# Two pieces of the next stage's start are issued in the third batch of an attention, not near its end

## The chip, the cores and the metric

The kernel runs on one NeuronCore of one Trainium2 chip. The metric is the device time of one execution in microseconds (us), as a median over executions. All arithmetic is in float32.

An instruction belongs to one engine: PE (TensorE, matrix products and transposes), DVE (VectorE), ACT (ScalarE), POOL (GpSimd) or SP (the queue that issues the DMAs). Each engine takes its instructions in one fixed order; an instruction that waits for another engine holds up everything behind it on its own engine.

## The reference

There are 8 sequences of 512 rows with 256 columns. Four blocks follow each other, each added to its input; the second and the fourth use the same weights.

```python
x = x + attn_a(layernorm(x))      # softmax attention with a low-rank key/value
x = x + ffn(layernorm(x))         # two layers: local attention, then a gated feed-forward
x = x + attn_b(layernorm(x))      # 16 heads of 16 columns, causal
x = x + ffn(layernorm(x))
```

The block around the change is `attn_b`. For every head and every pair of rows it computes

```python
dot    = q @ k.T
den    = |q|^2 + |k|^2 - 2 * dot + 1e-6
scores = dot * dot / den          # then the causal mask, softmax, times v, output projection
```

and `layernorm` of the block after it is `(x - mean) / sqrt(var + 1e-5)` over the 256 columns of each row.

## The kernel before, in words

The 8 sequences ("batches" in the code) are worked on in two groups of four. For a group, six kinds of stage follow each other: `attention_a`, then twice (local attention `attention_f`, `feedforward`), then `attention_b`, then twice again (`attention_f`, `feedforward`). So `attention_b` is run twice in the program, once for each group, and is followed each time by the first `attention_f` of the last block.

**How stages overlap.** Each stage gives a `head()`, a generator whose pieces prepare its first work, and a `run(ahead)`. While a stage runs, it calls `ahead()` at places of its own choosing; each call issues one piece of the next stage's head. When the pieces are used up, further calls do nothing. `ahead()` decides only where the instructions stand in the engines' orders; no call waits for anything by itself.

**The head of `attention_f`** runs its steps -5 to -1, one for each `ahead()` call, so five calls do something:

- Step -5: `statistics` of the first batch, that is `row_statistics`: for each of 4 row tiles one `bn_stats` (L276) and one `bn_aggr` (L277) on DVE into `st_f..` and `mv_f..`, then on POOL one `tensor_scalar` (L266) and one power (L267) that make `rstd_f..`.
- Step -4: `rows` of the first batch, that is `normalize_rows`: 4 `tensor_scalar` (L283) on DVE that write the tile `y_..` from `x`, `mv` and `rstd`.
- Step -3: `started`: a memset, 4 transposes of the first half of the columns on PE (`pht_f..`, L295) into the one PSUM buffer tagged `mm`, and a DVE copy out of it (`hT_f..`, L506).
- Step -2: the second half of the columns, the query, key and value products (`pqk_f..`, `pv_f..`, L510), the rotation (L538, L541, L552).
- Step -1: normalized and turned keys, the second tile's products, and `row_statistics` of the second batch.

**The steps of `attention_b`.** The work is cut into 22 units for each batch (2 for the first 128 rows, 4, 8 and 8 for the next), 88 for the four batches. Step `s` of 93 does a part of several units at once, in an order that is written out by hand in `each_part` and kept on every engine by `order_keeper`:

- PE: the products `den_b` of unit s and `dot_b` of unit s-1 (L1197), the first half of the transposes `ppt_b` of unit s-3 (L1269, into the `mm` buffer), a piece of other work or a filler product (`idle_b`, L1174), on odd steps the products with v (`o_b`, L1284) of two units, then the second half of the transposes.
- DVE: `refine` of unit s-1 (`r_b`, L1220), `highest` of unit s-2 (two L1239 for each pair of heads), copy of the first half of the transposes (`pt_b`, L1274), `error` of unit s (`t_b`, L1216), copy of the second half, then a piece if there is one.
- ACT: `inverse` of unit s (logarithm and exponential, `r_b` by the helper line L241), the square of `dot_b` (L1226), `exponentials` of unit s-2 (`num_b`, also L241).
- POOL: the mask of unit s-1 (L1232) and the sign of the row maxima of unit s-2 (`most_b`, L1249), for which the exponentials wait.

While batches 0, 1 and 2 are at work, the units of the batch after them are prepared by pieces in between: products `pu_b` (L1085, L1098), their squares on ACT (L1095) and their copies (L1111 on DVE, L1117 on ACT). The last batch has no such work beside it; there the places are filled with `idle_b`.

Where `ahead()` is called after a step, its DVE and POOL instructions are bound to come after that step's last one on the same engine. The PE and ACT instructions of the head are placed by the scheduler.

Of the kernel before, what the change touches and what calls it, by code (L numbers as in the profile page):

```python
# [46 lines left out]
def kernel(  # L47
# [56 lines left out]
    def part(flat, at, shape):  # L104

        n = int(np.prod(shape))
        view = flat[:, at : at + n]
        if len(shape) == 2:
            view = view.rearrange("p (k n) -> p k n", n=shape[1])
        return view, at + n  # L110
# [948 lines left out]
    def attention_b(batches, g, norms_b, state):  # L1059
# [107 lines left out]
        def whole(piece):  # L1167
            for part in piece[1:]:
                if part:
                    part()  # L1170
# [177 lines left out]
        def steps(ahead):  # L1348
# [5 lines left out]
            each, count = len(units) // len(batches), len(units)  # L1354
# [76 lines left out]
            for step in range(count + 5):  # L1431
                if step % each == 0:
                    with kept_order():
                        while prologues or norms:
                            whole((norms or prologues).popleft())
                    following = step // each + 1
                    if following < len(batches):
                        prologues = deque(stacks_and_values(batches[following]))
                elif step == 6:
                    norms.extend(Piece(False, dve=lambda part=part: part(batches[-1])) for part in norms_b)  # L1440
                made = len(nc.cur_bb.bb.instructions)
                with kept_order():
                    each_part(step)
                if step > count - 4:

                    after = len(nc.cur_bb.bb.instructions)
                    ahead[0]()
                    every = nc.cur_bb.bb.instructions
                    for engine in (mybir.EngineType.DVE, mybir.EngineType.Pool):
                        own = [i for i in every[made:after] if i.engine == engine]  # L1450
                        for i in every[after:] if own else ():
                            if i.engine == engine:
                                tc.add_manual_dep(i, own[-1].name, ISSUE_ORDER, reason="head")
                yield
# [3 lines left out]

        follower = []
        rest = steps(follower)  # L1460

        def head():
# [133 lines left out]
```

## Time and profile before

| | |
|---|---|
| median of 3 runs | 4423.52 us (4421.06 to 4423.76) |
| the profiled execution | 4422.09 us |
| its span, first to last instruction | 4420.3 us |
| mean granted TensorE clock | 0.993 |
| busy share of the span: PE, DVE, ACT, POOL | 95%, 70%, 61%, 27% |
| `attention_b` of the first group, about 1015 to 1500 us: PE, DVE, ACT, POOL busy of 485 us | 428.5, 443.3, 418.2, 123.9 us |
| `attention_b` of the second group, about 3213 to 3690 us: of 477 us | 423.5, 438.6, 415.2, 123.5 us |

How to read the views. Times are us from the span's start unless they are marked ns. A row of the timeline has start, length, engine, line of the kernel, operation, output<-inputs by the program's names, and how often it is repeated; in brackets stands how long the engine was idle before it and what ended that. PEld is the loading of PE's weights. A row of the windows has, after the stretch and its length, the busy time of PE, PEld, DVE, ACT and POOL (with the number of instructions), the TensorE clock that was granted (1.00 is full speed), the DMA engines' share and GB/s. The chain of waits follows back from the last instruction, at each step to what released it, and lists the pieces in order of time. The next instruction of an engine may start shortly before the one before it is shown to end, so the cost of an instruction in a busy stretch is the distance from its start to the next one's.

### The profile page before, as it was taken

The numbers are of one execution on the slowest core, as the hardware profiler recorded it, in microseconds if no ns is written. First come the engines' busy times: TensorE is split into PE (matmuls) and PEld (weight loads), VectorE is DVE, ScalarE is ACT, GpSimd is POOL, SyncE is SP. The second block draws the span as 40 slices with busy tenths as digits, with TensorE's granted clock in tenths as the row PEclk, the third lists the DMA queues.
The fourth block names the chain that finished last, engine by engine and source line by source line (L and its number), as shares of the span: only waits on it lengthen the run. The fifth ranks groups of instructions, "written<-read, shape, count | busy, mean of one in ns | idle before, by whom it ended". The sixth has DMA issues, their size and how long they took to land.

```text
span 4420.3 us, 70595 instructions
## 1 busy us (share of the span) xinstructions
PE 4195.3 (95%) x26580; PEld 2536.5 (57%) x26580; DVE 3100.1 (70%) x7497; ACT 2699.3 (61%) x6316; POOL 1175.5 (27%) x1220
## 2 busy tenths in 40 slices
PE   9999999999888899999999999999999888999999
PEld 5666556655555465566566665565545554655655
DVE  6678737747999786377466786377479997863773
ACT  6777517716898675176167675276178996742761
POOL 0014214312222342143200242243122223422431
PEclk9999999999999999999999999999999999999999
DMA  2000000000000000000100000000000000000000
GB/s 82 1 22 4 23 3 23 3 24 20 2 1 1 20 4 7 4 22 13 53 30 1 20 3 24 22 4 23 5 21 1 2 1 20 4 6 23 3 4 23
DMA packets 51092, 63.36 MB, mean 14 GB/s; under 512 B 6336, under 2 KB 45504, under 8 KB 50752
## 3 DMA queue, kind: packets, MB, share of 16 engines
q1 hardware_dynamic: 50752, 58.85, 4.1%
q8 instruction: 211, 3.46, 0.3%
q14 instruction: 129, 1.06, 0.1%
HBM read 46.28 MB, written 4.19 MB: 11 GB/s over the span
## 4 chain that ended last, share of the span: by engine, by line
PE 74%; DVE 14%; ACT 9%; issue 1%; POOL 1%; DMA 0%; SPq 0%; POOLq 0%; ACTq 0%; DVEq 0%
PE pu_g1x L932 3%; PE pu_g0x L932 3%; PE pu_g0y L932 3%; PE pu_g1y L932 3%; PE s_a L389 3%; PE o_a L425 3%; PE ppt_a L414 3%; PE pqk_f1x L510 2%; PE pqk_f1y L510 2%; PE pqk_f0y L510 2%; PE pqk_f0x L510 2%; DVE pt_b L1274 2%; PE ppt_b L1269 2%; DVE r_b L1220 2%; PE pu_b L1085 1%; DVE num_b L1239 1%
## 5 line engine op out<-in xcount | busy, mean ns | idle before, releaser
L1269 PE MATMUL ppt_b<-ident,num_b 128*128 128x128 f32 x1280 | 227.5, 294 | 93.1 <-DVE pt_b L1274 63.3
L1269 PEld LDWEIGHTS ppt_b<-ident,num_b 128*128 128x128 f32 x1280 | 139.7, 144 | 279.3 <-ACT num_b L241 92.6
L241 ACT ACTIVATE num_b<-num_b,most_b 128x512 f32<-128x512 f32 (+3 forms) x512 | 280.6, 553 | 21.4 <-POOL most_b L1249 21.2
L1232 POOL TENSOR_TENSOR num_b<-num_b,causal 128x256 f32<-128x256 f32 x256 | 200.8, 797 | 258.9 <-ACT num_b L1226 258.9
L1274 DVE COPY pt_b<-ppt_b 128x512 f32<-128x512 f32 (+1 forms) x352 | 224.4, 637 | 36.8 <-PE ppt_b L1269 35.3
L1239 DVE CUSTOM_DVE_ANT_0 num_b<-num_b,r_b 128x512 f32<-128x512 f32 (+3 forms) x512 | 238.1, 512 | 3.7 <-POOL num_b L1232 3.7
L241 ACT ACTIVATE p_a<-s_a,nm_a 128x512 f32<-128x512 f32 x256 | 173.7, 683 | 105.0 <-DVE nm_a L393 101.9
L1216 DVE TENSOR_TENSOR t_b<-den_b,r_b 128x1024 f32<-128x1024 f32 (+1 forms) x176 | 197.3, 1121 | 25.9 <-ACT r_b L241 25.6
L1197 PE MATMUL den_b<-st_b,st_b 18*128 18x384 f32 (+3 forms) x1024 | 207.0, 476 | 7.5 <-ACT yT_b L1075 4.1
L1220 DVE SCALAR_TENSOR_TENSOR r_b<-t_b,r_b 128x1024 f32<-128x1024 f32 (+1 forms) x176 | 208.6, 1185 | 0.2
L393 DVE TENSOR_REDUCE nm_a<-s_a 128x2 f32<-128x1024 f32 x128 | 156.4, 1223 | 70.4 <-PE s_a L389 70.4
L241 ACT ACTIVATE r_b<-den_b 128x1024 f32<-128x1024 f32 (+1 forms) x176 | 165.8, 942 | 52.5 <-PE den_b L1197 30.1
L241 ACT ACTIVATE p_f0y<-p_f0y,nm_f0y,rn_f0y 128x256 f32<-128x256 f32 (+1 forms) x256 | 143.8, 563 | 80.6 <-DVE nm_f0y L649 80.5
L241 ACT ACTIVATE p_f1y<-p_f1y,nm_f1y,rn_f1y 128x256 f32<-128x256 f32 (+1 forms) x256 | 143.8, 563 | 80.6 <-DVE nm_f1y L649 80.5
L1197 PE MATMUL dot_b<-st_b,st_b 16*128 16x384 f32 (+3 forms) x1024 | 191.6, 475 | 0.0
L241 ACT ACTIVATE p_f1x<-p_f1x,nm_f1x,rn_f1x 128x256 f32<-128x256 f32 (+1 forms) x256 | 143.8, 564 | 76.0 <-DVE nm_f1x L649 75.9
L241 ACT ACTIVATE p_f0x<-p_f0x,nm_f0x,rn_f0x 128x256 f32<-128x256 f32 (+1 forms) x256 | 143.8, 564 | 75.3 <-DVE nm_f0x L649 75.2
L407 ACT ACTIVATE p_a<-p_a,sums_a 128x512 f32<-128x512 f32 x256 | 171.9, 719 | 26.5 <-DVE sums_a L405 26.5
L552 POOL TENSOR_TENSOR ro_f1x<-ro_f1x,rs_f1x 128x512 f32<-128x512 f32 x64 | 80.2, 1276 | 360.8 <-DVE rs_f1x L541 144.8
L552 POOL TENSOR_TENSOR ro_f0x<-ro_f0x,rs_f0x 128x512 f32<-128x512 f32 x64 | 80.2, 1275 | 360.6 <-DVE rs_f0x L541 144.8
L241 ACT ACTIVATE r_b<-r_b 128x1024 f32<-128x1024 f32 (+1 forms) x176 | 172.5, 980 | 5.7
L1226 ACT ACTIVATE num_b<-dot_b 128x1024 f32<-128x1024 f32 (+1 forms) x176 | 164.8, 937 | 3.1 <-PE dot_b L1197 3.1
(356 smaller groups left out, 11238.9 us busy)
## 6 DMA issues: line engine op xcount, KB each, us to landing
x<-in_x SPq DMA_DIRECT2D x8, 512.0 KB
out<-x SPq DMA_DIRECT2D x8, 512.0 KB
wf_0x<-in_f_wqkv SPq DMA_DIRECT2D x2, 1536.0 KB
wf_0y<-in_f_wqkv SPq DMA_DIRECT2D x2, 1536.0 KB
wf_1x<-in_f_wqkv SPq DMA_DIRECT2D x2, 1536.0 KB
wf_1y<-in_f_wqkv SPq DMA_DIRECT2D x2, 1536.0 KB
wg_0x<-in_f_w SPq DMA_DIRECT2D x2, 1386.0 KB
wg_0y<-in_f_w SPq DMA_DIRECT2D x2, 1386.0 KB
```

Of the source, the lines that this page charges most:

```text
L241: i = nc.scalar.activation(out, in_, func, **more).ins
L407: nc.scalar.activation(p[:, odd], p[:, odd], AF.Identity, scale=some[:, odd : odd + 1])
L510: nc.tensor.matmul(dst.rearrange("p h d -> p (h d)"), lhsT=hTs[b][:, k, t * P : (t + 1) * P], rhs=wqkv[:, k, c * INNER : (c + 1) * INNER], ...
L932: nc.tensor.matmul(pu[: cols.stop - cols.start, c], lhsT=w1[:, k, cols], rhs=hT[:, k, :], start=(k == 0), stop=(k == 1),)
L1197: return nc.tensor.matmul(s[:, a, m * width : (m + 1) * width], lhsT=left[at, j, past:width], rhs=right[at, j, :width], start=True, stop=True,
L1216: nc.vector.tensor_mul(t[:, :, :cols], den[:, :, :cols], r[:, :, :cols])
L1220: nc.vector.scalar_tensor_tensor(r[:, :, :cols], t[:, :, :cols], 2.0, r[:, :, :cols], ALU.subtract, ALU.mult)
L1226: nc.scalar.activation(num[:, :, :cols], dot[:, :, :cols], AF.Square, scale=-0.5)
L1232: nc.gpsimd.tensor_add(own, own, causal.unsqueeze(1).to_broadcast([P, 2, P]))
L1239: nc.vector.tensor_tensor_reduce(out=s4[:, a, m, :], in0=s4[:, a, m, :], in1=r4[:, a, m, :], scale=-1.0, scalar=LOWEST, op0=ALU.mult, op1= ...
L1269: nc.tensor.transpose(ppt[:, k, :], p[:, a, k * P : (k + 1) * P], ident)
L1274: nc.vector.tensor_copy(pt[:, a, :nblocks, :], ppt[:, :nblocks, :])
```

## The change

`attention_b`'s `steps` calls `ahead` after eight of its steps, as before. Before, these are the last eight of the 93 steps (85 to 92). Now they are steps 53 and 57 and the last six (87 to 92). Steps 53 and 57 lie in the third batch, whose units start in steps 44 to 65.

```diff
                 made = len(nc.cur_bb.bb.instructions)
                 with kept_order():
                     each_part(step)
-                if step > count - 4:
+                if step > count - 2 or step in (count - 35, count - 31):
 
                     after = len(nc.cur_bb.bb.instructions)
                     ahead[0]()
```

`count` is 88. The pieces are handed out in their own order, so the head's step -5 moves from step 85 to step 53, its step -4 from 86 to 57, and its steps -3, -2 and -1 stay after steps 87, 88 and 89. The last three calls do nothing, before and after. Both runs of `attention_b` are changed in the same way.

## The prediction

> **What bounds the kernel now.** I read the page first, then the windows of the two `attention_b` stages, then the chain of waits at the end of the first of them and the timelines of PE, DVE, ACT and POOL around steps 85 to 88 (about 1469 to 1495 us) and steps 53 to 59 (about 1316 to 1344 us). PE is busy 95% of the span, but that is an average. In `attention_b` DVE, PE and ACT are nearly level, and whichever is late passes it on.
>
> The chain at the end of the first `attention_b`:
>
> ```profile
> 1472.95 0.60 DVE pt_b L1274
> 1473.55 0.66 DVE st_f0y L276 x2
> ...
> 1474.99 0.08 DVE mv_f0y L277
> 1475.08 1.11 DVE r_b L1220
> ...
> 1477.47 0.61 DVE pt_b L1274
> 1478.09 0.14 issue
> 1478.22 0.90 PE ppt_b L1269 x4
> ```
>
> So the row statistics lie on the path: `refine` comes after them, then the copy, and PE waits for that copy. The timelines show what this does to PE and POOL, and where the normalized rows lie:
>
> ```profile
> 1478.22 0.90 PE L1269 MATMUL ppt_b<-ident,num_b 128*128 128x128 f32 x4 [3.04 <-DVE pt_b L1274]
> 1476.99 1.36 POOL L267 TENSOR_TENSOR rstd_f0y<-rstd_f0y,neg_half 128x4 f32<-128x4 f32 x1
> 1478.43 0.19 POOL L1249 TENSOR_SCALAR most_b<-most_b 128x2 f32<-128x2 f32 x1
> 1479.77 1.37 DVE L283 TENSOR_SCALAR y_0y<-x,mv_f0y,rstd_f0y 128x256 f32<-128x256 f32 x4
> 1486.20 0.69 DVE L1274 COPY pt_b<-ppt_b 128x512 f32<-128x512 f32 x1 [0.97 <-PE ppt_b L1269]
> ```
>
> PE stood still for 3.04 us, and the clock fell behind it. The windows, at the tail and, for comparison, in the third batch:
>
> ```profile
> 1475.20:1478.20 3.00, 0.00 (x0) 0.01 (x1) 3.00 (x8) 1.54 (x2) 1.75 (x2) 1.00 0.00 0
> 1478.20:1485.20 7.00, 6.98 (x46) 3.57 (x50) 7.00 (x13) 5.50 (x10) 2.00 (x6) 0.52 0.01 2
> 1300.00:1350.00 50.00, 47.21 (x380) 23.24 (x376) 46.17 (x95) 45.41 (x91) 10.50 (x22) 1.00 0.00 1
> ```
>
> Where the pieces go to, PE has 2.8 us to spare in 50, DVE 3.8, ACT 4.6. That is no slack for a piece; the question is which engine is late at the exact place:
>
> ```profile
> 1316.22 0.95 DVE L1220 SCALAR_TENSOR_TENSOR r_b<-t_b,r_b 128x768 f32<-128x768 f32 x1
> 1318.74 0.52 PE L1269 MATMUL ppt_b<-ident,num_b 128*128 128x128 f32 x3 [0.58 <-DVE pt_b L1274]
> 1319.48 0.61 ACT L241 ACTIVATE num_b<-num_b,most_b 128x384 f32<-128x384 f32 x1
> ```
>
> PE already waits 0.58 us for DVE there.
>
> **What moves.** The order of the built programs differs, for each stage, in this: 4 L276, 4 L277 (DVE) and L266, L267 (POOL) go from before `refine` of step 86 to before `refine` of step 54 (the last L277 just behind it); 4 L283 go from before `refine` of step 87 to before that of step 58. As a consequence PE has the first `pht` transposes before the last `dot_b` instead of behind it, and the first two `pqk` products before the second `ppt_b` instead of behind it; DVE has the first `hT` copy (L506) before both `highest` of its step instead of between them. No DMA and nothing on SP or ACT moves. The amount of work is the same.
>
> **Gain at the end of a stage.** Start to start, one DVE step of that place is 1.13 (`refine`) + 2 x 0.61 (`highest`) + 0.60 + 1.13 (`error`) + 0.60 = 4.68 us. The starts of `refine` are 1468.78, 1474.99, 1481.05 and 1486.81: three steps took 18.03 us. In the second group they run from 3667.13 to 3685.17, 18.04 us. Without the pieces DVE needs 3 x 4.68 = 14.04, so 4.0 us go: 1.53 (statistics up to 1474.99), 0.09 (the last L277), 1.28 (rows, 1479.77 to 1481.05), and 1.1 that is the wait of 0.97 for PE at 1486.20 and some rounding. PE can follow: its wait of 3.04 shrinks by 1.6 to about 1.4. Waits of 1.36 to 1.37 at the like place of step 82 (1456.85, 3655.20) left the clock at 1.00, so I take it that the clock no longer falls here. What is late next is DVE itself.
>
> Behind that, the reordered PE work. From the `refine` of step 88 to the second `hT` copy the second group took 3691.74 - 3685.17 = 6.57 us. Now the first `hT` copy comes 0.6 earlier, but 0.95 us of `pqk` stand ahead of the second `ppt_b`; I get 6.8, a loss of 0.2 (between a gain of 0.4, if `pqk` fits the wait, and a loss of 0.95). The first group took 1494.50 - 1486.81 = 7.69, since the clock was at half there a second time (1488.7 to 1492.1); if that goes too, 1.1 is gained once (0 to 1.1; I take 1.1, as only the first group shows this fall). Both stages: 8.0 - 0.4 + 1.1 = 8.7 us gained.
>
> **Cost in the third batch.** Before step 54's `refine` 1.53 us of DVE are put in (1316.22). Queued behind them are `refine`, `highest`, and the copy for which PE waits at 1318.74: PE is late by the full 1.53. On POOL L266 and L267 stand ahead of `most_b` and wait for the last L277, behind `refine`. At step 86 `most_b` came 2.3 us after that L277; here that is about 1321.0, and the exponentials that start at 1319.48 start at about 1321.2. ACT's L1117 and PE's `pp_b` (1321.50, which waits for L1117) follow. Cost 1.6 us (1.5 to 1.8). Before step 58's `refine` 1.28 us are put in (1334.12). There the chain of waits runs over PE and ACT, and DVE waits 0.31 and 0.58 us for `r_b` at 1336.80 and 1342.12; but PE's second `ppt_b` and with it `den_b` move too. Cost 0.7 (0.3, what passes both waits, to 1.28). Both stages: 2 x 2.3 = 4.6 us.
>
> **The clock there.** PE's wait at 1318.74 becomes 0.58 + 1.53 = 2.11 us. The trace has like waits in these stages. Behind 2.07 us (ended 1036.65 and 3234.72) the clock fell to half both times, for 6.8 us; behind 2.46 (1157.94) it fell for 3.4 us; behind 2.50 (1274.95, 3473.48) it did not. Three of five: likelier than not. Half clock doubles the matmul rows: 4 `ppt_b` take 1.08 instead of 0.63 us, `idle_b` 1.91 instead of 1.02. In the 5.7 us that follow (the mean of those three) PE is on the chain for some 3.3 us (`pp_b`, `o_b`, `ppt_b`, 1321.50 to 1324.81), elsewhere ACT or DVE is. So a fall costs about 1.7 us (0.9, if half is hidden, to 3.4, 6.8 us all on the chain).
>
> [...]
>
> **Sum.** -8.7 + 4.6 + 2 x 1.7 = -0.7 us with a fall in both stages, -2.4 with one, -4.1 with none. The profiled execution took 4422.09 us, 1.8 above its span and 1.4 below the median of 4423.52. The forecast on the median is 4423.5 - 0.7 = 4422.8 us. About 0.2% (8.8 us) is what a measurement of this kernel can tell from no change.
>
> **Rivals.**
>
> *Full clock at step 54 in both stages* (0.22): -4.1, so 4419.4 us. For it: 2.50 us without a fall, twice. Against: 2.07 with one, twice.
>
> *The pieces are hidden in the third batch* (0.12): DVE is idle 0.41 + 0.79 + 0.45 + 0.31 + 0.58 = 2.5 us between 1316 and 1344, and 2.9 are put in. If all that idle time is usable, a stage pays 0.4, and the sum is -8.7 + 0.8 = -7.9; with the reordered tail at its better end (1.2 better) -9.1: 4414.4 us. Against: at 1318.74 PE waits for DVE, not the reverse.
>
> *The new half-clock stretches feed themselves* (0.16, slower): a slow PE makes ACT and DVE late, and these leave PE new waits. It decides when a stage loses over (8.8 + 4.1) / 2 = 6.5 us, some 13 us of half clock with PE on the chain: two of the longest falls of this trace (6.8 us) one after the other. For it: the first group's second fall, 3.4 us after its first. Against: the batch has filler products, and no stretch of the trace is that long. Its price, two such stretches in each stage: 4 x 3.4 - 4.1 = +9.5, so 4433.0 us.
>
> *The change does nothing*: excluded, both pieces stand elsewhere in the built program.
>
> **Numbers.** The forecast, a fall in at least one stage, has 0.50. It and the full-clock case lie within 0.2%: 0.72. Faster by more: 0.12 (hidden). Slower by more: 0.16. The range from 4415 to 4431 holds the first two with their bounds and about half of each of the others.
>
> **What would show it.** Right: the starts of `refine` at steps 85 to 88 are 4.7 us apart and the clock stays at 1.00 behind step 86; `refine` of step 54 comes 1.5 us later, PE's wait there is about 2.1 us, and the next batch starts 2 to 4 us later. Wrong: PE's wait at step 54 stays under 1 us or DVE's idle time vanishes there (hidden); the clock falls at the tail all the same (the gain is 2 to 3 us smaller for each stage); or the stage loses more than 5 us between steps 54 and 66 (fed by itself).

## The result, and the profile after

The changed kernel takes 4431.03 us (median, 4422.35 to 4433.8), the kernel before 4422.12 us (4420.38 to 4424.54): a ratio of 1.002 with a 95% interval of 1.0014 to 1.0026, 8.9 us slower. The forecast was 4422.8 us, 0.7 us less than before; the measured median is 8.2 us above it.

In the profiled execution of the changed kernel (4433.8 us, the longest of its 20; span 4432.0, mean granted clock 0.991) the busy times are as before, but for PE: 4206.9 us, 11.6 more for the same products. That is the clock: a *fall* is, from here on, the granted clock going from 1.00 to 0.50 for a while. In `attention_b` and what follows it directly the stretches at half clock add up to some 82 us, before to some 61; 20 us more at half speed are, by estimate, some 10 us more of PE for the same products.

The end of the stage, where the statistics were. The chain of waits of the changed kernel:

```profile
1478.42 1.13 DVE r_b L1220
...
1482.51 0.60 DVE pt_b L1274
1483.11 1.13 DVE r_b L1220
...
1486.08 0.14 issue
1486.21 0.63 PE ppt_b L1269 x4
```

Nothing stands between the copy and `refine` any more. The timeline (start, length, engine, line, operation, idle time before it) has the four starts of `refine`, of steps 85 to 88:

```profile
1478.34 1.21 DVE L1220 SCALAR_TENSOR_TENSOR r_b<-t_b,r_b 128x1024 f32<-128x1024 f32 x1
1483.02 1.22 DVE L1220 SCALAR_TENSOR_TENSOR r_b<-t_b,r_b 128x1024 f32<-128x1024 f32 x1
1487.71 1.22 DVE L1220 SCALAR_TENSOR_TENSOR r_b<-t_b,r_b 128x1024 f32<-128x1024 f32 x1
1493.28 1.22 DVE L1220 SCALAR_TENSOR_TENSOR r_b<-t_b,r_b 128x1024 f32<-128x1024 f32 x1
```

They are 4.68, 4.69 and 5.57 us apart; before it was 6.21, 6.06 and 5.76. The first two are the forecast step, the third is 0.9 too long. PE and ACT in the timeline of the same kernel, at step 54, at step 86 and in the next stage's first products:

```profile
1323.17 0.52 PE L1269 MATMUL ppt_b<-ident,num_b 128*128 128x128 f32 x3 [2.14 <-DVE pt_b L1274]
1332.13 0.56 DVE L1274 COPY pt_b<-ppt_b 128x384 f32<-128x384 f32 x1 [2.94 <-PE ppt_b L1269]
1486.21 0.63 PE L1269 MATMUL ppt_b<-ident,num_b 128*128 128x128 f32 x4 [1.47 <-DVE pt_b L1274]
1500.77 4.51 PE L510 MATMUL pqk_f0y<-wf_0y,hT_f0y 128*128 128x512 f32 x6 [1.26 <-DVE hT_f0y L506]
```

The waits are as forecast: 2.14 us at step 54 (forecast 2.11), 1.47 at step 86 (forecast 1.4, before 3.04). What follows them is not. The windows, with the granted clock third from the end:

```profile
1324.10:1330.90 6.80, 6.80 (x29) 3.81 (x31) 3.59 (x8) 5.16 (x12) 1.22 (x3) 0.50 0.00 0
1378.70:1382.10 3.40, 3.40 (x11) 2.61 (x9) 3.40 (x7) 3.37 (x6) 0.73 (x2) 0.50 0.00 0
1389.00:1395.80 6.80, 6.80 (x73) 4.48 (x71) 5.27 (x9) 5.07 (x9) 1.71 (x5) 0.50 0.01 2
1402.60:1406.00 3.40, 3.21 (x37) 2.18 (x37) 3.40 (x18) 3.00 (x8) 1.82 (x2) 0.50 0.02 5
1487.90:1491.30 3.40, 3.37 (x20) 1.84 (x22) 3.40 (x7) 3.31 (x4) 0.42 (x2) 0.51 0.02 5
1501.60:1505.00 3.40, 3.40 (x5) 1.35 (x4) 0.00 (x0) 1.61 (x3) 0.00 (x0) 0.50 0.00 0
```

Half clock behind step 54, three times around the batch boundary (the start of the fourth batch, steps 66 to 71; before once, 1389.7 to 1396.5), and twice at the end of the stage. In the last row DVE did nothing at all: PE alone is on the path, the six `pqk` products took 4.51 us, and at full clock they take 2.81. The second group shows the same six (3525.7, 3580.3, 3590.6, 3604.2, 3689.5, 3703.2).

**Where the time went.** The same DVE instructions are compared in both traces, and the start after less the start before is followed through the stage. Its steps, in us:

| | forecast | group 1 | group 2 |
|---|---|---|---|
| statistics ahead of step 54's `refine` | 1.6 | 1.54 | 1.53 |
| half clock behind step 54 | 1.7 | 2.94 | 3.00 |
| rows ahead of step 58's `refine`, less what the next waits give back | 0.7 | 1.29 - 0.84 | 1.29 - 0.83 |
| batch boundary | 0 | 1.79 | 1.93 |
| end of the stage, to the `refine` of step 88 | -4.0 | -3.10 | -3.20 |
| from there to the first rotation (L538) | -0.9, 0.2 | 0.68 | 1.79 |
| sum | -0.9, 0.2 | 4.3 | 5.5 |

Both sums make 9.8 us, near the 8.9 of the medians. (The two profiled executions differ by 11.7: 2.9 more arose ahead of the first third batch, 2.3 of them at the program's start, and 1.0 less between the two stages' ends and third batches.)

### The profile page after: what moved, and what is told of

Same layout as the page of the kernel before. It is cut to its first block, busy times and chain, and to the rows that moved or that the text cites. A ratio compares the mean times of both kernels' runs of the same rounds, so it can differ in the third digit from the quotient of the medians.

```text
span 4432.0 us, 70595 instructions
## 1 busy us (share of the span) xinstructions
PE 4206.9 (95%) x26580; PEld 2542.0 (57%) x26580; DVE 3096.6 (70%) x7497; ACT 2699.8 (61%) x6316; POOL 1175.6 (27%) x1220
## 4 chain that ended last, share of the span: by engine, by line
PE 75%; DVE 13%; ACT 9%; issue 1%; POOL 1%; DMA 0%; SPq 0%; POOLq 0%; ACTq 0%; DVEq 0%
PE pu_g1x L932 3%; PE pu_g0x L932 3%; PE pu_g0y L932 3%; PE pu_g1y L932 3%; PE s_a L389 3%; PE o_a L425 3%; PE ppt_a L414 3%; PE pqk_f1x L510 2%; PE pqk_f0y L510 2%; PE pqk_f1y L510 2%; PE ppt_b L1269 2%; PE pqk_f0x L510 2%; DVE pt_b L1274 2%; DVE r_b L1220 2%; PE den_b L1197 1%
## 5 line engine op out<-in xcount | busy, mean ns | idle before, releaser
L1269 PE MATMUL ppt_b<-ident,num_b 128*128 128x128 f32 x1280 | 226.7, 293 | 90.3 <-DVE pt_b L1274 67.7
L1269 PEld LDWEIGHTS ppt_b<-ident,num_b 128*128 128x128 f32 x1280 | 139.1, 144 | 277.6 <-ACT num_b L241 89.3
L1274 DVE COPY pt_b<-ppt_b 128x512 f32<-128x512 f32 (+1 forms) x352 | 223.9, 636 | 46.3 <-PE ppt_b L1269 44.9
```

What stands on the lines that cost most here:

```text
L1269: nc.tensor.transpose(ppt[:, k, :], p[:, a, k * P : (k + 1) * P], ident)
L1274: nc.vector.tensor_copy(pt[:, a, :nblocks, :], ppt[:, :nblocks, :])
```

## The experiments

All times are medians, in us; the kernel before was measured beside each of them at 4421.9 to 4422.8. Each trace is of one execution, which need not be the median one. The diffs show the main lines only. Three tools are used: filler products (nothing reads them; one costs 0.86 us of PE) in an existing wait of PE, the pieces moved singly, and pure delay.

**1. Filler products in the wait of step 54.** Into the changed kernel, behind step 54's projection:

```diff
+ for _ in range(2 if step == count - 34 else 0):
+     nc.tensor.matmul(whole_pu[:, 1], lhsT=ident, rhs=w[:, 0, :], start=True, stop=True)
```

> The changed kernel, with two more filler products (identity times the projection weights, 128 x 256, into an unused half of a tile; nothing reads them) placed in PE's 2.14 us wait of step 54 in both groups. Theory A (the fall of the clock at step 54 is the larger part of the cost): no half clock at 1324.1 to 1330.9 nor at its place in the second group, the copy after it is no longer 2.94 us late, 2 x 2.9 us come back, and some of the half clock at the batch boundary goes with it: about 6 us less than the changed kernel, near 4425. Theory B (the extra DVE and POOL work in the third batch is the cost, the clock only shows it): the clock stays up but the time stays within 2 us of the changed kernel, near 4431.

Measured: 4424.25, 6.8 below the changed kernel. The windows of this kernel, and its wait in the timeline (L1274 here is L1269 of the changed kernel):

```profile
1318.00:1331.00 13.00, 12.16 (x76) 6.09 (x74) 11.79 (x29) 9.48 (x18) 3.67 (x7) 1.00 0.00 0
```
```profile
1321.19 0.52 PE L1274 MATMUL ppt_b<-ident,num_b 128*128 128x128 f32 x3 [0.43 <-DVE pt_b L1279]
```

PE does more work and the stage is shorter: with the statistics still there (+1.53 us at `refine`), the step behind it grows by 0.19 us, not 2.94. So the 2.9 us are the clock's and no queue's. Theory B falls.

**2. The price alone.** The kernel before, with the same two pieces made once more in steps 53 and 57 (results unused, kept in their place as `ahead`'s pieces are), its end untouched:

```diff
+ if step == count - 35: spare["got"] = row_statistics([xs[batches[0]]], "spare")
+ if step == count - 31: normalize_rows([xs[batches[0]]], [scratch], *spare.pop("got"))
```

> The kernel before, with its end of the stage untouched, and the statistics and the normalized rows of the first batch made once more, unused, in steps 53 and 57. So this has the price in the third batch and no gain at the end. Theory A: 1.5 (statistics) + 1.3 (rows) + 2.9 (fall of the clock) = 5.7 us for each stage, some more at the batch boundary: 11 to 14 us over the kernel before, 4433 to 4436, so that the end of the stage had gained only 3 to 5 us in all. Theory B (no price of the clock of its own): 2 x 2.5 = 5 us, 4427, which would mean that the end of the stage lost time by the change.

Measured: 4434.92, ratio 1.0027 (1.0018 to 1.0036), 13.0 above the kernel before. The trace has 6.6 us in the first stage and 6.9 in the second: 1.5, 2.9, 1.3 - 0.8, and 1.7 and 1.9 at the batch boundary. The changed kernel is 8.9 above before, so its end of the stage gained 4 us in all, and not the forecast 8.7.

**3. The statistics moved, the rows left behind step 86.**

```diff
- if step > count - 2 or step in (count - 35, count - 31):
+ if step > count - 3 or step == count - 35:
```

> The changed kernel, but only the statistics are made in step 53; the normalized rows stay behind step 86, as before. Theory A: the fall at step 54 stays, the 1.29 us of the rows in the third batch go and come back at the end of the stage: within 2 us of the changed kernel, near 4430. Rival (the rows are what is dear, since they come when DVE has lost its slack): 3 to 4 us less than the changed kernel, near 4427.

Measured: 4422.79, below both expectations. The fall behind step 54 is there (2.93 us in each stage). The rows' 0.45 us could not make 8; the trace shows the batch boundary 1.08 and 0.98 us *shorter* than before, with one stretch of 3.4 us of half clock, where the changed kernel has three.

**4. Filler products at the end of the kernel before, one step too early** (three in the idle piece of step 85, whose following wait is only 0.39 us).

> The kernel before, with three more filler products in the idle piece of step 85, in PE's 3.04 us wait (two groups). Theory A (what the end of the stage loses is the half clock behind the wait): no half clock at 1478.4 to 1485.3, the wait of 0.97 us for PE goes, and the second fall of the first group with it: 2 x 1.1 + 1.1 = 3 us less than before, 4419 to 4420. Theory B (DVE sets the end of the stage, PE's clock is hidden there): within 1 us of before.

Measured: 4422.93, no difference that can be told. PE's long wait was still 2.88 us; the products only made the step 1.9 us longer, and half clock behind it lasted 3.4 us, not 6.8. It tests neither theory.

**5. Statistics alone and the filler products of step 54.**

> Statistics alone in step 53, rows behind step 86 as before, and the two filler products in PE's wait of step 54: the two cures of the runs before taken together. Theory A (the 2.9 us of half clock behind step 54 and the rows in the third batch are two separate costs): 2 x 2.9 us less than the kernel with the statistics alone (4422.8), so 4417, about 5 us less than the kernel before. Rival (both cures only move the work against a fixed grid of the clock's falls, and the falls go elsewhere): 4421 to 4424.

Measured: 4423.06: the rival holds. Step 54 was cured (0.19), but in the first stage the clock fell behind the wait of 1.37 us of step 82 (1460.3 to 1463.7, cost 1.6), where it had stayed up before, and the boundary cost 0.4 and 0.5 more than before.

**6. Step 54 and one filler product ahead of the wait of 1.47 us of step 86.**

> The changed kernel with the two filler products in step 54 and one more filler product (0.86 us) in the idle piece ahead of PE's wait of 1.47 us of step 86, both groups. Theory A (at the end of the stage the half clock behind that wait eats what the shorter DVE steps gain): no half clock behind 1.47 us, 1 to 2 us less for each stage than with the filler products of step 54 alone (4424.3): 4420 to 4422. Rival (DVE sets the pace at the end of the stage and the half clock there is hidden): 4424, and the starts of refine stay 4.7 us apart as they are.

Measured: 4424.94, no gain over the first run. The time and the `refine` starts (4.69 us apart) are the rival's, its reason is not: half clock isn't hidden here. The wait of 1.47 us is gone from the trace, but the clock fell behind that of step 82 (1462.0, 3660.2; 1.6 us each), and further on (1489.3, 3687.5; 1.5 us in the second group).

**7. Three filler products directly ahead of the 3.04 us of the kernel before.**

```diff
- return Piece(False, first=lambda: kept_awake(ps_s.tile([P, 2, 4, P], F32, tag="s", name=f"idle_b{s}")))
+ def awake():
+     space = ps_s.tile([P, 2, 4, P], F32, tag="s", name=f"idle_b{s}")
+     for _ in range(1 + {-2: 3}.get(s - count, 0)):
+         kept_awake(space)
+ return Piece(False, first=awake)
```

> The kernel before with three more filler products (2.6 us) in the idle piece directly ahead of PE's wait of 3.04 us (the run before put them one step too early, where they only made the step longer). Theory A: no half clock behind it, the wait of 0.97 us at the last refine goes, and the first group's second fall: 3 us less than before, 4419. Rival (hidden): within 1 us of before, 4421 to 4423.

Measured: 4418.0, ratio 0.999 (0.9981 to 0.9999): 4.5 us below the kernel before, with an interval that just excludes no change. The timeline and the window of what had been at half clock:

```profile
1475.62 3.60 PE L1174 MATMUL idle_b<-wb,ident 128*128 128x512 f32 x8
1479.68 0.63 PE L1269 MATMUL ppt_b<-ident,num_b 128*128 128x128 f32 x4 [0.46 <-DVE pt_b L1274]
```
```profile
1478.20:1485.20 7.00, 5.65 (x53) 2.71 (x51) 7.00 (x17) 4.51 (x7) 2.61 (x6) 1.00 0.01 2
```

In the first group this end of the stage took 2.2 us less. In the second the profiled execution (4422.5, the longest of the 11) lost 2.3 us to two falls further on, at 3684.8 and 3691.6.

**8. The changed kernel with all work from step 32 on later** (three filler products in the like piece of the second batch).

> The changed kernel with three more filler products (2.6 us of PE) in step 32, the like place of the second batch, in both groups: all work behind it is some 2 us later, nothing else changes. In the traces so far all falls of the clock within one run start on a grid of 3.413 us. Theory G (where a fall comes depends on how the work lies on this grid): with the work moved by about half a grid step, other waits are met; the stretches of half clock at the batch boundary and at the end of the stage (1378.7, 1402.6, 1501.6 in the changed kernel) come or go, and the time moves by something other than the added 2 x 2 us. Rival (the falls belong to the waits): the same stretches behind the same waits, 2 x 2 us more than the changed kernel, 4435.

Measured: 4436.45, 5.4 above the changed kernel for 2 x 2.57 us of products. The total speaks for the rival, the places do not: in place of the falls at 1378.7, 1402.6 and 1501.6 there are others behind 2.50 us (1276.2), 1.70 (1388.9), 2.29 (1399.1) and 1.37 (1467.4) and one past step 88 (1494.7), and the fall behind 1.47 us of step 86 did not come in either group. The cost that left one place came in at another.

**9 to 11. All named waits filled, in the changed kernel and in the kernel before; the boundary alone in the changed kernel.** The idle pieces of steps 66 and 68 get one and three more products (`{-22: 1, -20: 3}`). Run 9 has also two in step 54 and one in step 86; run 10, three in step 86.

> The changed kernel with filler products in all the waits of PE that were named so far: two in step 54, one and three in the idle pieces ahead of the waits of 1.70 and 3.00 us at the batch boundary, one ahead of the wait of 1.47 us at the end of the stage, in both groups. Theory A (what the change costs over its work is half clock): none of these places is at half clock, and the changed kernel comes below the kernel before: the forecast's work terms alone give -8.7 + 4.6 = -4 against a kernel before that is treated alike (the next run). Rival (the change is worth nothing even at full clock): within 1 us of the next run or above it.

> The kernel before, treated in the same way: one and three more filler products at the batch boundary, three ahead of the wait of 3.04 us at the end of the stage. Theory A: the 6.8 us of half clock at the boundary go as well as those of the end of the stage, 1 to 2 us less for each stage than with the end of the stage alone (4418.0): 4414 to 4416. Rival (the falls move to the next wait): 4418.

> The changed kernel with the filler products at the batch boundary alone (ahead of 1.70 and 3.00 us); the wait of step 54 and the end of the stage as they are. Theory A (the three stretches of half clock at the boundary cost 1.8 to 1.9 us for each stage more than the one of the kernel before): 4 to 6 us less than the changed kernel, 4425 to 4427; the fall at step 54 stays. Rival (they are hidden, DVE sets the pace of the boundary): 4430 to 4432.

Measured: 4418.77 (run 9), 4421.72 (run 10, 4416.0 to 4427.4), 4425.37 (run 11). The boundary of the kernel before, the changed one and run 11, each in the 45 us from the same place of the work:

```profile
1359.00:1404.00 45.00, 38.11 (x397) 25.38 (x396) 41.53 (x98) 38.25 (x82) 12.98 (x25) 0.92 0.01 1
```
```profile
1367.00:1412.00 45.00, 39.38 (x388) 26.01 (x388) 39.84 (x94) 36.27 (x78) 12.59 (x24) 0.85 0.00 1
```
```profile
1366.00:1411.00 45.00, 40.97 (x406) 26.22 (x404) 42.28 (x100) 38.92 (x82) 14.26 (x25) 0.96 0.00 1
```

The changed kernel does less in that time (DVE 39.84 of 45 us, not 41.53) at a lower clock (0.85, not 0.92); filled, at 0.96, DVE does 42.28. Filling the boundary is worth 5.7 us to the changed kernel, filling step 54 was worth 6.8; all together 12.3 (run 9), more than the loss of 8.9. So the loss goes when the waits are filled, although run 9 still has falls at the ends of its stages (1487.6 and 1494.4; 3689.2) and one at the second boundary (3600.4). Run 10 is above both of its expectations: the second group's end of the stage came out 3.7 us longer than that of before, with falls behind the next waits (3679.9 behind 1.34 us, 3690.2 behind 1.25), the rival's mechanism at more than its price. With both kernels so filled, the changed one is 3 us less; the intervals of both against the kernel before (0.9983 to 1.0001, 0.9993 to 1.0011) overlap, so this is not settled, and it is no less than run 7.

**12. The kernel before with its work 1.7 us later from step 32 on** (two products).

> The kernel before, unchanged but for two more filler products in step 32 of each group, which make all work behind them 1.7 us later (three cost 2.57 us in the run of the changed kernel). In the traces so far the cost of the batch boundary goes with the place of the work on the 3.413 us grid of the clock's falls (start of the refine at 1359.3 less the phase of the grid): 0.3 to 1.2: nothing; 1.35 to 1.5: -1.0; 2.0 to 2.3: +1.7 to +1.9 with three stretches of half clock; 2.4 to 2.9: +0.5 to +0.7 with two. Before has 0.34 and 0.68 there. Theory G: with its work 1.7 us later the unchanged kernel comes to about 2.0 in the first group, and has there three stretches of half clock in place of one, from 1371 on, and 1.7 us more at the boundary; in the second group the place is read from the trace and the cost follows the same steps. Time 4422.5 + 3.4 for the products + 2 to 4 for the boundaries = 4428 to 4430. Rival (the extra stretches at the boundary come from the statistics and rows in the third batch): one stretch of 6.8 us as before, boundary cost 0, 4426.

Measured: 4428.1, ratio 1.0012 (1.0003 to 1.0021): 6.0 above before, for 3.4 us of products. That is within what the grid theory expected, but the profiled execution (4423.6, the lowest of them) doesn't show the place aimed at: it lay at 0.98 and 0.85 us, and had one stretch and a boundary cost of -0.3 and -0.1. The rule on the place held; that an unchanged kernel is slowed so by delay alone is not shown.

**The grid.** Within each run, the starts of all half-clock stretches are multiples of 3.4133 us apart, to within 0.011 us (17 of them in the changed kernel: 1040.8, 1074.9, 1150.0, 1324.1, ...), and the stretches last one or two such steps, 3.413 or 6.827 us (but for the one that the program's end cuts off). With the phase of that grid read from a run, the place of the work on it is the start of the third batch's `refine` at 1359.3 (3557.8) of before, less the phase, modulo 3.413. The 22 stages without fillers at the boundary, in the order of that place:

| place on the grid, us | stages | half clock at the boundary | cost there against before |
|---|---|---|---|
| 0.27 to 1.23 | 9, before among them | 6.8 | -0.3 to 0.2 |
| 1.35 to 1.51 | 2 (run 3) | 3.4 | -1.1 and -1.0 |
| 1.97 to 2.33 | 4 (run 2, the changed kernel) | 3.4 + 6.8, mostly + 3.4 | 1.65 to 1.95 |
| 2.42 to 2.85 | 6 (runs 5, 6, 8, 1) | 3.4 + 6.8 | 0.5 to 0.7 |
| 3.33 | 1 (run 5) | 6.8 | 0.4 |

So in these stages the boundary's cost goes with where its work lies on the grid, across edits: the changed kernel's work lay at 2.04 and 2.33 us, that of before at 0.34 and 0.68. The rows were drawn after the costs were known, and no run put the unchanged kernel's work into the third one.

A single wait shows it more cleanly. PE's wait of 1.37 us at step 82 is in all 28 stages of the fourteen traces: in the five where it began 0.08 to 0.23 us behind a point of the grid the clock fell, in the 23 where it began 0.70 to 2.88 us behind one it did not. The wait of 1.47 us at step 86 is in twelve stages: a fall in the six where it began 3.33 to 0.49 us (that is, around a point of the grid), none in the six at 0.88 to 1.68.

Beside the place, the traces show how busy PE was in each *grid step*, the 3.413 us from one point of the grid to the next. Take all grid steps at full clock of the fourteen traces, and PE's busy time in them without the products of 16 and 18 rows (`dot_b`, `den_b`). Where it was under 0.34 of the grid step, a fall followed in all 100; where it was 0.46 or more, in none of 17439; between the two, in 70 of 279 (in the two traces of before and the changed kernel: 19 of 19, none of 2486, 11 of 36). With these products counted as busy the traces have no such border: falls came behind grid steps that were busy for up to 0.97 (at 1484.2 in run 9), and none behind others at 0.42 (in the two traces: up to 0.77, and 0.45). The place alone does not settle the cost: the boundaries of run 11 lay at 2.14 and 2.15, as in the third row, but filled, and cost -0.8 and -0.1.

## Why the prediction was wrong

The sum was -0.7 us and the two stages of the traces make 9.8. Of the 10.5 between them 4.9 are at the ends of the stages, 3.7 at the batch boundaries and 2.5 in the price of the fall of step 54; the statistics and the rows cost 0.6 less than forecast.

**The moves and the waits: right.** The statistics cost 1.54 us (forecast 1.6), the rows 0.45 net (0.7), PE's wait at step 54 was 2.14 us (2.11). The DVE steps at the end shrank to 4.68 us. Nothing on SP, POOL or ACT mattered: `most_b` came after the power, as forecast, and ACT's exponentials started no later than the statistics alone make it.

**"Likelier than not" a fall at step 54: right, and its price 1.7: wrong.** It fell in all ten stages that have the wait unfilled (the changed kernel, runs 2, 3, 8 and 11), at 2.9 to 3.0 us each. In all ten the wait began 0.11 to 0.69 us behind a point of the grid; what it does elsewhere on the grid no run shows. The working counted only PE's instructions on the chain for the mean stretch of 5.7 us; but the stretch was 6.8 us each time, and the copies and refinements queued behind PE's late transposes all moved by the whole of it (DVE stood 2.94 us at 1332.13). The upper bound of 3.4 held. This term is short by 1.2 to 1.3 us a stage.

**"I take it that the clock no longer falls here": wrong, the largest error.** It rested on two waits of 1.36 to 1.37 us that left the clock up. The trace of before had the counter-example, a wait of 1.46 us at step 22 of the second group, with 6.8 us of half clock behind it (the same wait of the first group, at 1146.42, had none):

```profile
3344.48 0.63 PE L1269 MATMUL ppt_b<-ident,num_b 128*128 128x128 f32 x4 [1.46 <-DVE pt_b L1274]
3345.50:3352.30 6.80, 6.80 (x70) 4.58 (x70) 5.10 (x8) 5.89 (x12) 2.47 (x5) 0.50 0.01 2
```

In the changed kernel it fell behind 1.47 us in both groups, and behind 1.26 us in the `pqk` products again. In all twelve stages whose end is the changed one (the changed kernel, runs 1, 6, 8, 9 and 11) at least one stretch of half clock lies there. Where it lies past step 88, `refine` gained the forecast 4.0 us (runs 8, 9 and 11), so the DVE sum itself was right; but the stretch is then paid for behind it (1.5 to 1.7 us from there to the first rotation in their second groups, forecast 0.2). The second fall of the first group did go (1.03 us up to the second `hT` copy, forecast 1.1), and one that costs 1.7 came behind it, in the `pqk` products (1501.6). From the `refine` of step 84 to the first rotation the changed kernel gained 2.4 and 1.4 us, against a forecast of 4.9 and 3.8; the two stages together lack 4.9 us.

**The batch boundary: not in the sum at all.** The forecast took the shift of the third batch as passing through what follows unchanged. It costs 1.8 and 1.9 us there, and run 11, which fills the waits of the boundary, is 5.7 us below the changed kernel (more than the 3.7, as it fills also what was at half clock before the change).

**The rivals.** The slower one ("half-clock stretches feed themselves", 4433.0) gave the time best and names the clock as the cause, but that its number is near is luck: it priced two stretches of 6.8 us behind step 54 in each stage, and there is one. Its mechanism is not what the runs show: the new stretches at the boundary are no longer ones fed by the fall of step 54, since in runs 1, 5 and 6, without that fall, there are two of them in four of six stages, and in run 3, with it, one. They go with the place on the grid. "Hidden" is excluded by 1.54 us at `refine`; "full clock" by falls in both stages, and in all ten with this wait.

**The failing step's root.** In the changed kernel waits of 1.26 to 2.15 us were followed by half clock. The forecast had unequal outcomes for like waits before it (2.07 us with a fall, 2.50 without one), and still took one outcome for the length of the wait at the end of the stage.

**Open.** Between 0.34 and 0.46 of a grid step, counted as above, the traces don't settle which ones a fall follows. No run changes the number of `dot_b` and `den_b` products alone: that a border shows when they are left out is a fit to these traces, and what they do to the clock is not shown. In the two stages of the changed kernel the grid steps ahead of a fall were busy for 0.37 to 0.77 with all products counted, and others at 0.45 to 0.57 were followed by none. The one ahead of 1378.7 was busy for 2.62 of 3.40 us, without a wait over 0.8 us; 1.61 us of it are `dot_b` and `den_b`.

## What to carry to other kernels

Where PE waits a microsecond or two at a time and the trace shows the granted clock falling, a move that makes one wait shorter and another longer isn't priced by DVE's or PE's own durations: list every wait near the path that is as long as those a fall came behind (here from 1.25 us, run 10, and one fall without a wait over 0.8), before and after, and price each as a possible fall, here of 3.4 or 6.8 us of half clock. In these runs the outcome went with the place on the grid (step 82's wait: a fall at 0.08 to 0.23 us behind a point, none at 0.70 to 2.88). Carry the shift on through all such places behind it, not only the ones edited. The cheaper cure is to leave the work where it was and put spare products in the wait: three ahead of the 3.04 us brought 4.5 us against the kernel before (4418.0 against 4422.5), where moving the work out of that wait cost 8.9. With the boundary filled as well (run 10) that gain was not seen (4421.72), since falls came behind the next waits.

## What was not expected of the hardware

- All falls of the clock in one run start on a common grid of 3.4133 us (to 0.011 us), and behind one wait the clock fell or not with its place: behind the 1.37 us of step 82 it stayed at full speed in the kernel before and the changed one, and fell in both groups of runs 6 and 8 and in the first of run 5.
- A fall came without a long wait: at 1378.7 the longest one in the 3.4 us ahead was 0.8 us. A busy PE did not exclude a fall: one came behind a grid step in which it was busy for 2.62 of 3.40 us (1378.7), and one behind 0.97 of a grid step, mostly with products of 16 and 18 rows (run 9, 1487.6).
- More work was less time: two unused products in each stage took 6.8 us off the changed kernel; the same kind of product where PE doesn't wait cost its full 0.86 us.
